# Graph layer on one core: the layers cut into five parts, merges ten chunks later, and all edge rows gathered by the POOL queue

## The chip, the core and the metric

The kernel runs on one core of a Trainium2 chip. The core has five engines with instruction queues of their own: PE (TensorE, matrix products), DVE (VectorE, elementwise work and reductions), ACT (ScalarE, activations), POOL (GpSimd, here only issuer of indirect DMAs) and SP (SyncE, here only issuer of plain DMAs). The metric is device time in microseconds, the median of the runs; lower is better. Before the change it is 1955.35 us (three runs, 1953.97 to 1955.7).

## The reference

```python
def reference(x, src, dst, Wg, Ws, bg, W1, b1, W2, b2, W3, b3):
    z = jnp.maximum(_layernorm(x, axis=-1), 0.0)        # x: 12500 x 128, fp32
    msgs = z[src]                                       # 200000 edges; src is random
    agg = segment_sum(msgs, dst, num_segments=12500)    # dst is sorted
    deg = segment_sum(ones, dst, num_segments=12500)
    agg = agg / jnp.maximum(deg, 1.0)[:, None]
    h = jax.nn.relu(agg @ Wg + z @ Ws + bg)             # 128
    h = jnp.tanh(h @ W1 + b1)                           # 512
    h = jnp.tanh(h @ W2 + b2)                           # 512
    return x + h @ W3 + b3                              # 128
```

Every edge needs one row of `z` (512 bytes), picked by `src`; the rows of edges with the same `dst` are added up.

## The kernel before

**Head (lines 120 to 274).** POOL first issues 80 indirect DMAs (line 141), each of which gathers 128 rows of the raw `x`; these 80 chunks of edges are normalised after they are gathered. Meanwhile the layer norm of all of `x` is computed and written to a table `htab` in DRAM.

**Edge loop (lines 586 to 634).** The 200000 edges are cut into 1563 chunks of 128, `c` in the loop. A chunk's rows lie in a tile of 128 x 128. `gather(c)` (line 296) is one indirect DMA on POOL that brings the 128 rows from `htab` into one of 32 tiles of the pool `rows_in` (`AHEAD = 32`), up to 32 gathered chunks ahead of the chunk in work. `onehot` builds on DVE, for eight chunks at a time, a matrix that says which of about 144 neighbouring nodes each edge belongs to. `add(c)` multiplies rows by that matrix on PE, and so sums the edges per node into PSUM. The PE queue is written out in program order (`keep_in_program_order`, line 285), and so is SP's (line 294).

**Three kinds of chunks.** 80 are the raw ones of the head. 21 are in the list `slow` (every 59th from chunk 72 on, below chunk 1376): their rows are fetched by SP, one row per DMA, 128 DMAs per chunk in batches of 16 (`row_loads`, lines 315 to 333); SP first loads the row addresses into registers, which `places` has loaded and DVE has multiplied by 512 (line 312). The other 1462 are gathered by POOL.

**Blocks.** The nodes are cut into 28 blocks: 23 of 512, then 256, 128, 128, 128 and 84. A block of 512 takes 64 chunks. Chunks whose window spans two blocks are summed into a PSUM tile `edge`, copied to SBUF by ACT (`sums`, line 427), and added to both blocks by `merge` (line 443, two matmuls with the identity). `merge(b)` stands two chunks after the block's last chunk. Then `layers(b)` (line 498) is put on the list `work`: it is a generator, and each `yield` is a step, mostly one matmul of the layers. Below chunk `QUICK = 1376` one step is taken every second chunk (line 629). From there on a small plan decides: `there` (line 612) is the time at which the plan takes the chunk's rows to be there, and layer steps that fit before it go first (lines 613 and 614). At chunk 1376 the plan's clock is far behind `there`, and so all steps left of the block in work are written out at once.

**Other inputs of the layers.** `own(s)` (line 460) loads by SP the block's rows of `x` (`xb`, three buffers) and of `htab` (`hb`, one buffer); `own_turned(s)` turns `hb` on PE. `store` issues the outputs on SP at least 12 chunks after they were computed.

Of the kernel before, what the change touches and what calls it, by code (L numbers as in the profile page):

```python
# [20 lines left out]
F32 = mybir.dt.float32  # L23
BF16 = mybir.dt.bfloat16
I32 = mybir.dt.int32
U8 = mybir.dt.uint8
AF = mybir.ActivationFunctionType
ALU = mybir.AluOpType
# [3 lines left out]
P = 128  # L32
EPS = 1e-5
CPR = 16
BLK = 512
PIECE = 14
GRP = 8
NRAW = 10
RAW0 = 256
STEP = 40  # L40
AHEAD = 32
SLOW0 = 72
EACH = 58
LOADS = 16
LATE = 12
QUICK = 1376

# [10 lines left out]
def windowed(ctx, tc, x, src, dst, Wg, Ws, bg, W1, b1, W2, b2, W3, b3, out, flag):  # L58
    nc = tc.nc
    N, D = x.shape  # L60
    (E,) = src.shape
    H = W1.shape[1]
    HM = H // P
# [6 lines left out]
    NCH = -(-E // P)  # L70
# [8 lines left out]
    def raw(c):  # L79
        return RAW0 <= c < RAW1 and (c - RAW0) % STEP < GRP  # L80


    slow, n = [], 0
    for c in range(SLOW0, QUICK):
        if not raw(c):
            if n == 0:
                slow.append(c)
                n = EACH
            else:
                n -= 1  # L90


    def first(w, span=per):
# [8 lines left out]
    blocks, n = [], 0  # L102
# [7 lines left out]
    raws = ctx.enter_context(tc.tile_pool(name="raws", bufs=1))  # L110
    rows_one = ctx.enter_context(tc.tile_pool(name="rows_one", bufs=2))
    rows_in = ctx.enter_context(tc.tile_pool(name="rows_in", bufs=AHEAD))
# [9 lines left out]
    for t, a in ((rsrc, src), (rdst, dst)):  # L122
        a = a[RAW0 * P : RAW1 * P].rearrange("(u e) -> u e", u=NRAW)[:, : GRP * P]
# [14 lines left out]
    for g in range(NRAW):  # L138
        t = raws.tile([P, GRP, D], F32, name=f"raw{g}")
# [44 lines left out]
    with tc.tile_pool(name="setup", bufs=1) as sp, tc.tile_pool(name="ln", bufs=2) as ln:  # L184
# [59 lines left out]
        for c0, w in WINDOWS[1:]:  # L244
            v = low[:, c0:]
# [47 lines left out]
    def sp_dma(*a):  # L293
        tc.keep_in_program_order(nc.sync.dma_start(*a))  # L294
# [8 lines left out]

    ROWB = 4 * D
    hbytes = htab.rearrange("n d -> (n d)").bitcast(U8)

    def places(c):

        ix = ed.tile([1, P], I32, name="ix", bufs=2)
        sp_dma(ix, src[c * P : (c + 1) * P].rearrange("(o p) -> o p", o=1))  # L310
        at = ed.tile([1, P], I32, name="at", bufs=2)
        nc.vector.tensor_scalar(at, ix, float(ROWB), None, op0=ALU.mult)
        return at

    def row_loads():
        nxt_at = places(slow[0])
        for i, c in enumerate(slow):
            at = nxt_at
            if i + 1 < len(slow):
                nxt_at = places(slow[i + 1])  # L320
            r = rows_one.tile([P, D], F32, name="srows")
            rows_t[c] = r
            rb = r.bitcast(U8)
            for p0 in range(0, P, LOADS):
                loads, vs = nc.values_load_multi_w_load_instructions(
                    at[:, p0 : p0 + LOADS], engines=[mybir.EngineType.SP], min_val=0, max_val=(N - 1) * ROWB,
                    skip_runtime_bounds_check_because="src holds rows of x, as the indirect DMAs take it to",
                )
                for ld in loads:
                    tc.keep_in_program_order(ld)  # L330
                for p, v in enumerate(vs, p0):
                    sp_dma(rb[p : p + 1, :], hbytes[bass.ds(v, ROWB)].rearrange("(o b) -> o b", o=1))
                yield

    def raw_stats(i):
# [124 lines left out]
    def own(s):  # L460

        n0 = s * BLK
        n = min(BLK, N - n0)
        k, whole = -(-n // P), n // P
        xb = ml.tile([P, BLK // P, D], F32, name="xb", bufs=3)
        if whole < k:
            nc.vector.memset(xb[:, whole, :], 0.0)
        if whole:
            sp_dma(xb[:, :whole, :], x[n0 : n0 + whole * P, :].rearrange("(t p) d -> p t d", p=P))
        if whole < k:  # L470
            sp_dma(xb[: n - whole * P, whole, :], x[n0 + whole * P : n0 + n, :])
        hb = ml.tile([P, BLK // P, D], F32, name="hb", bufs=1)
        sp_dma(hb[:, :k], htab[n0 : n0 + k * P, :].rearrange("(t p) d -> p t d", p=P))
        owns[s] = (hb, xb)

    def own_turned(s):

        k = -(-min(BLK, N - s * BLK) // P)
        hb, xb = owns.pop(s)
        pt = ps_t.tile([P, BLK // P, P], F32, name="pt")  # L480
        for t in range(k):
            pe.transpose(pt[:, t, :], hb[:, t, :], ident)
        hT = ml.tile([P, BLK], F32, name="hT")
        nc.scalar.copy(hT[:, : k * P], pt[:, :k, :].rearrange("p t n -> p (t n)"))
        hTs[s] = (hT, xb)

    def own_part(b):

        n0, n = blocks[b]
        whole = n // P  # L490
        xb = ml.tile([P, -(-n // P), D], F32, name=f"xs{b}", bufs=1)
        if whole:
            sp_dma(xb[:, :whole, :], x[n0 : n0 + whole * P, :].rearrange("(t p) d -> p t d", p=P))
        if n > whole * P:
            sp_dma(xb[: n - whole * P, whole, :], x[n0 + whole * P : n0 + n, :])
        xss[b] = xb

    def layers(b):


        n0, n = blocks[b]
        s, off = divmod(n0, BLK)
        hT, xb = hTs[s]
        k, whole = -(-n // P), n // P
        rest = n - whole * P
        if n != BLK:
            xb = xss.pop(b)
        mm, hop = 4 * (n / 2400 + 0.003), 0.5 + n / 1200

        size, bufs = (P, 2) if n <= P else (BLK, 1)  # L510
        yield 0, 0
# [3 lines left out]
        p0 = flat(ps_m.tile([P, 4, P], F32, name="pm"))  # L515
        pe.matmul(p0[:, :n], ws, hT[:, off : off + n], start=True, stop=False)
        yield mm, n / 90
        pe.matmul(p0[:, :n], wg, mT[:, :n], start=False, stop=True)
        h0 = ml.tile([P, BLK], F32, name="h0")
        nc.scalar.activation(h0[:, :n], p0[:, :n], AF.Relu, bias=bgc)  # L520
        yield 0, 0
        h1 = ml.tile([P, HM, size], F32, name=f"h1_{size}", bufs=bufs)
        for m in range(HM):
            yield mm, hop if m == 0 else 0
            p1 = flat(ps_m.tile([P, 4, P], F32, name="pm"))
            pe.matmul(p1[:, :n], w1[:, m * P : (m + 1) * P], h0[:, :n], start=True, stop=True)
            nc.scalar.activation(h1[:, m, :n], p1[:, :n], AF.Tanh, bias=b1c[:, m : m + 1])  # L527
        h2 = ml.tile([P, HM, size], F32, name=f"h2_{size}", bufs=bufs)
        for m in range(HM):
            p2 = flat(ps_m.tile([P, 4, P], F32, name="pm"))  # L530
            for kk in range(HM):
                yield mm, hop if m == 0 and kk == HM - 1 else 0
                pe.matmul(
                    p2[:, :n], w2[:, kk, m * P : (m + 1) * P], h1[:, kk, :n], start=(kk == 0), stop=(kk == HM - 1)
                )
            nc.scalar.activation(h2[:, m, :n], p2[:, :n], AF.Tanh, bias=b2c[:, m : m + 1])  # L536
        p3 = flat(ps_m.tile([P, 4, P], F32, name="pm"))
        for kk in range(HM):
            yield mm, hop if kk == HM - 1 else 0
            pe.matmul(p3[:, :n], w3[:, kk, :], h2[:, kk, :n], start=(kk == 0), stop=(kk == HM - 1))  # L540
        h3 = ml.tile([P, BLK], F32, name="h3", bufs=1)
        nc.scalar.activation(h3[:, :n], p3[:, :n], AF.Identity, bias=b3c)  # L542
        yield 0, 0
        yield k * 0.225, hop
# [11 lines left out]

    order = [c for c in range(NCH) if not raw(c) and c not in slow]
    loading = row_loads()
    work, done, nxt, behind = [], 0, 0, 0
# [8 lines left out]
    def soonest():  # L568
        two = work[: 2 if len(work) > 1 and work[1][3] < work[0][3] else 1]
        return min(two, key=lambda w: max(w[2], now), default=None)  # L570

    def go_on(w):
        nonlocal now
        if w:
            now = max(now, w[2]) + w[1]
            w[1:] = *next(w[0], (None, 0)), w[3] + 1
            w[2] += now
            if w[1] is None:
                work.remove(w)
# [6 lines left out]
    for c in range(NCH):  # L586
# [15 lines left out]
        while nxt < len(order) and nxt < behind + AHEAD:  # L602
            gather(order[nxt])
            nxt += 1
        if not raw(c) and c not in slow:
            behind += 1
            batch = behind * P // (EACH * LOADS)
            if behind > SLOW0 - 2 * EACH and batch > (behind - 1) * P // (EACH * LOADS):
                next(loading, 0)
        if c >= QUICK:  # L610

            there = 12.0 + 1.25 * (NRAW * GRP + order.index(c)) if c not in slow else 0
            while soonest() and max(now, soonest()[2]) < there:
                go_on(soonest())
            now = max(now, there) + 0.27
        add(c)

        if done < len(blocks) and (c - 2 if across[done] else c) == reach[done][-1]:
            if across[done]:
                merge(done)  # L620
            work.append([layers(done), 0, 0, 0])
            done += 1
# [391 lines left out]
```

## Time and profile before

| what | value |
|---|---|
| median of three runs | 1955.35 us |
| the profiled execution's own time | 1952.27 us |
| its span, first to last instruction | 1950.5 us (1.77 us lie around it) |
| PE busy, matmuls | 1354.8 us (69%), 5213 instructions |
| DVE busy | 1069.7 us (55%) |
| ACT busy | 231.8 us (12%) |
| POOL busy | 1458.0 us (75%), 1550 instructions |
| indirect gathers of rows, on POOL | 1462, 944 ns each |
| single-row loads, on SP | 2688, 0.5 KB each |
| mean granted PE clock | 0.916 |

A matmul in fp32 shows as two instructions in the profile. "Idle before" is the time that an engine stood still just ahead of an instruction, and the releaser is what ended it; "issue" means that nothing which the profile shows was waited for. The chain that ended last is followed back from the last instruction to whatever released each step.

### The profile page before, as it was taken

The page shows a single profiled execution, that of the slowest core. Times are in us where ns is not written, and L with a number is a line of the kernel's source. Part 1 is how long each engine was busy: PE and PEld are TensorE (multiplying, and loading weights), DVE is VectorE, ACT ScalarE, POOL GpSimd, SP SyncE. Part 2 cuts the span into 40 slices and gives each one's busy share as a digit, 9 for nine tenths or more (in the row PEclk, how much of TensorE's full clock was granted, in tenths as well). Part 3 has the DMA queues.
Part 4 walks back from the last instruction along what each step waited for, and adds up shares of the span by engine and source line. Part 5 has one row for each costly group of instructions (what it writes and reads, how often), then busy time and mean ns, then how long its engine had stood idle before and what let it go on. Part 6 is the DMA issues. An engine that isn't in the chain of part 4 may idle for free.

```text
span 1950.5 us, 20753 instructions
## 1 busy us (share of the span) xinstructions
PE 1354.8 (69%) x5213; PEld 803.5 (41%) x5213; DVE 1069.7 (55%) x671; ACT 231.8 (12%) x364; POOL 1458.0 (75%) x1550
## 2 busy tenths in 40 slices
PE   0057387778787787776676677677776676778797
PEld 0034253444454444433333334343343343454466
DVE  7874874655666566645445445455455454545430
ACT  1100211101111011101011001010110101101122
POOL 7777777777777777777777777777777777777774
PEclk9999689899899989999999998989889889868797
DMA  7822222222222222222222222222222222222221
GB/s 199 231 77 65 54 70 54 70 65 60 71 70 71 64 60 70 70 54 71 70 54 70 54 71 70 54 71 65 60 70 54 71 70 53 77 69 61 55 63 38
DMA packets 125595, 139.78 MB, mean 72 GB/s; under 512 B 33169, under 2 KB 99958, under 8 KB 125272
## 3 DMA queue, kind: packets, MB, share of 16 engines
q0 software_dynamic: 49344, 101.16, 20.5%
q1 hardware_dynamic: 72962, 33.90, 6.3%
q10 hardware_dynamic: 3160, 3.31, 0.6%
q8 instruction: 43, 0.70, 0.2%
q14 instruction: 86, 0.70, 0.1%
HBM read 125.43 MB, written 12.82 MB: 71 GB/s over the span
## 4 chain that ended last, share of the span: by engine, by line
issue 36%; DMA 26%; PE 24%; POOL 11%; DVE 1%; ACT 0%; SPq 0%; POOLq 0%; DVEq 0%; ACTq 0%
DMA rows<-htab,scol 26%; PE pm L285 12%; PE agg L285 8%; POOL rows L298 7%; POOL raw L141 4%; PE edge L285 3%; PE pt L288 1%; DVE oh L362 0%; DVE shared L171 0%; DVE raw L172 0%; DVE shared L175 0%; ACT sq L174 0%; DMA raw<-in_x_dram,rsrc 0%; SPq L294 0%; DVE rd L399 0%
## 5 line engine op out<-in xcount | busy, mean ns | idle before, releaser
L298 POOL DMA_INDIRECT rows<-htab,scol x1462 | 1379.5, 944 | 445.8 <-issue 293.4
L285 PE MATMUL agg<-oh,rows 128*128 128x144 f32 (+3 forms) x2096 | 543.9, 358 | 331.5 <-DMA rows<-htab,scol 327.7
L285 PEld LDWEIGHTS agg<-oh,rows 128*128 128x128 f32 x2096 | 369.4, 217 | 711.4 <-DMA rows<-htab,scol 595.0
L285 PE MATMUL pm<-h,w 128*128 128x512 f32 (+3 forms) x1344 | 614.1, 553 | 0.2
L362 DVE TENSOR_TENSOR oh<-shared,dloc 128x1152 f32<-128x1152 f32 (+2 forms) x186 | 245.2, 1322 | 622.5 <-PE agg L285 420.3
L372 DVE TENSOR_REDUCE cnt<-oh 128x200 bf16<-128x1600 f32 (+2 forms) x186 | 523.6, 2825 | 7.9 <-DMA htab<-h 3.6
L285 PE MATMUL edge<-oh,rows 128*128 128x144 f32 (+2 forms) x828 | 211.9, 347 | 131.3 <-DMA rows<-htab,scol 130.4
L285 PEld LDWEIGHTS edge<-oh,rows 128*128 128x128 f32 x828 | 139.8, 206 | 264.6 <-DMA rows<-htab,scol 216.9
L285 PEld LDWEIGHTS pm<-h,w 128*128 128x128 f32 x1344 | 212.7, 197 | 11.8 <-issue 9.8
L536 ACT ACTIVATE h<-pm,b2c 128x512 f32<-128x512 f32 (+3 forms) x112 | 70.8, 632 | 649.1 <-PE pm L285 649.1
L141 POOL DMA_INDIRECT raw<-in_x_dram,rsrc x80 | 77.6, 970 | 25.5 <-issue 23.8
L527 ACT ACTIVATE h<-pm,b1c 128x512 f32<-128x512 f32 (+3 forms) x112 | 70.2, 632 | 182.1 <-PE pm L285 181.5
L399 DVE RECIPROCAL rd<-rd 128x512 f32<-128x512 f32 (+3 forms) x28 | 81.8, 2920 | 0.0
L513 DVE TENSOR_TENSOR mT<-agg,rd 128x512 f32<-128x512 f32 (+3 forms) x28 | 17.3, 619 | 90.5 <-PE agg L285 90.5
L200 PE MATMUL pm<-ident,idx_f 98*128 98x98 f32 x32 | 6.2, 376 | 76.3 <-DVE agg L179 42.7
L285 PE MATMUL agg<-sums,ident 128*128 128x140 f32 (+3 forms) x108 | 28.4, 412 | 27.5 <-ACT sums L427 27.5
L397 DVE TENSOR_SCALAR rd<-pm 128x512 f32<-128x512 f32 (+3 forms) x28 | 17.4, 621 | 52.4 <-PE pm L285 52.4
L520 ACT ACTIVATE h<-pm,bgc 128x512 f32<-128x512 f32 (+3 forms) x28 | 17.7, 632 | 236.4 <-PE pm L285 236.4
L542 ACT ACTIVATE h<-pm,b3c 128x512 f32<-128x512 f32 (+3 forms) x28 | 17.7, 632 | 184.5 <-PE pm L285 184.5
L285 PE MATMUL pm<-hT,ws 128*128 128x512 f32 (+3 forms) x56 | 38.6, 784 | 0.0
L285 PEld LDWEIGHTS agg<-sums,ident 128*128 128x128 f32 x108 | 25.4, 309 | 28.3 <-ACT sums L427 28.3
L200 PEld LDWEIGHTS pm<-ident,idx_f 98*128 98x128 f32 x32 | 5.1, 223 | 77.1 <-issue 42.9
(70 smaller groups left out, 497.4 us busy)
## 6 DMA issues: line engine op xcount, KB each, us to landing
srows<-htab SPq DMA_DIRECT2D x2688, 0.5 KB
rows<-htab,scol POOLq DMA_INDIRECT x1462
xb<-in_x_dram SPq DMA_DIRECT2D x24, 256.0 KB
hb<-htab SPq DMA_DIRECT2D x24, 256.0 KB
out_dram<-o SPq DMA_DIRECT2D x23, 256.0 KB
htab<-h SPq DMA_DIRECT2D x6, 896.0 KB
xt<-in_x_dram SPq DMA_DIRECT2D x5, 896.0 KB
raw<-in_x_dram,rsrc POOLq DMA_INDIRECT x80
```

Source lines behind the costliest of these rows:

```text
L141: nc.gpsimd.indirect_dma_start(out=t[:, j, :], out_offset=None, in_=x, in_offset=bass.IndirectOffsetOnAxis(ap=rsrc[:, g, j : j + 1], axis=0),)
L285: tc.keep_in_program_order(nc.tensor.matmul(*a, **k))
L288: tc.keep_in_program_order(nc.tensor.transpose(*a, **k))
L298: nc.gpsimd.indirect_dma_start(out=r, out_offset=None, in_=htab, in_offset=bass.IndirectOffsetOnAxis(ap=scol[:, c : c + 1], axis=0),)
L362: nc.vector.tensor_tensor(oh[:, :k, :w], lane[:, None, :w].to_broadcast([P, k, w]), dloc[:, g * GRP : g * GRP + k][:, :, None].to_broadcas ...
L372: nc.vector.tensor_reduce(cnt[:, :n], shifted, AX.X, ALU.add)
L397: nc.vector.tensor_scalar(rd[:, :m], dg[:, :m], 1.0, None, op0=ALU.max)
L399: nc.vector.reciprocal(rd[:, :m], rd[:, :m])
L520: nc.scalar.activation(h0[:, :n], p0[:, :n], AF.Relu, bias=bgc)
L527: nc.scalar.activation(h1[:, m, :n], p1[:, :n], AF.Tanh, bias=b1c[:, m : m + 1])
L536: nc.scalar.activation(h2[:, m, :n], p2[:, :n], AF.Tanh, bias=b2c[:, m : m + 1])
L542: nc.scalar.activation(h3[:, :n], p3[:, :n], AF.Identity, bias=b3c)
```

## The change

- The list `slow`, `places` and `row_loads` go: SP loads no rows. All 1483 chunks that are not raw are gathered by POOL, in the same order, with the same 32 tiles.
- `layers` is cut into five parts: `part0` (the mean, `ws`, `wg`, relu), `part1` (`w1`), `part2` (`w2`), `part3` (`w3`) and `part4` (turn back, add `x`, hand the store on). For a block that is done well before chunk 1376, the order is part 0 of this block, part 3 of the block before, part 1, part 4 of the block before, part 2. Later blocks go through all five parts in a row; the first of them starts with what is left of the block before.
- `merge` and the start of the layers come ten chunks after the block's last chunk (`LEAD = 10`) rather than two; from chunk 1376 on still two.
- `xb` is loaded when `part0` starts (`own_part`) instead of with `hb`, with two buffers instead of three.
- The plan's arrival time from chunk 1376 on is 7.5 + 1.251 per gather instead of 12.0 + 1.25, and two blocks are in work side by side only where the first is a quick one of at most 128 nodes.

```diff
-SLOW0 = 72
-EACH = 58
-LOADS = 16
 LATE = 12
+LEAD = 10
...
-    rows_one = ctx.enter_context(tc.tile_pool(name="rows_one", bufs=2))
...
-    def places(c):
...
-    def row_loads():
...
-                for p, v in enumerate(vs, p0):
-                    sp_dma(rb[p : p + 1, :], hbytes[bass.ds(v, ROWB)].rearrange("(o b) -> o b", o=1))
-                yield
...
-        xb = ml.tile([P, BLK // P, D], F32, name="xb", bufs=3)
...
+        if n == BLK:
+            xb = ml.tile([P, BLK // P, D], F32, name="xb")
+        else:
+            xb = ml.tile([P, -(-n // P), D], F32, name=f"xs{b}", bufs=1)
...
+    def layers(b, before):
+        part = lambda f, *a: lambda: f(*a)
+        last = [] if before is None else [part(part3, before), part(part4, before)]
+        if reach[b][-1] + LEAD < QUICK:
+            return one_by_one(
+                part(part0, b), *last[:1], part(part1, b, True), *last[1:], part(part2, b)
+            )
+        return one_by_one(
+            *last, part(part0, b), part(part1, b, False), part(part2, b), part(part3, b), part(part4, b)
+        )
...
-    order = [c for c in range(NCH) if not raw(c) and c not in slow]
-    loading = row_loads()
+    order = [c for c in range(NCH) if not raw(c)]
...
-        two = work[: 2 if len(work) > 1 and work[1][3] < work[0][3] else 1]
+        two = work[: 2 if len(work) > 1 and work[1][3] < work[0][3] and work[0][4] else 1]
...
-            there = 12.0 + 1.25 * (NRAW * GRP + order.index(c)) if c not in slow else 0
+            there = 7.5 + 1.251 * (NRAW * GRP + order.index(c))
...
-        if done < len(blocks) and (c - 2 if across[done] else c) == reach[done][-1]:
+        lead = LEAD if c < QUICK else 2
+        if done < len(blocks) and (c - lead if across[done] else c) >= reach[done][-1]:
             if across[done]:
                 merge(done)
-            work.append([layers(done), 0, 0, 0])
+            quick = reach[done][-1] + LEAD >= QUICK
+            before = done - 1 if done and reach[done - 1][-1] + LEAD < QUICK else None
+            work.append([layers(done, before), 0, 0, 0, quick and blocks[done][1] <= P])
             done += 1
```

More of the change, by code (lines that the diff above doesn't have):

```diff
@@ L25 @@
 I32 = mybir.dt.int32
-U8 = mybir.dt.uint8
 AF = mybir.ActivationFunctionType
@@ L80, in raw @@
         return RAW0 <= c < RAW1 and (c - RAW0) % STEP < GRP
[L83 to L90, printed above, removed]
     def first(w, span=per):
@@ L302, in gather @@
         rows_t[c] = r
-    ROWB = 4 * D
-    hbytes = htab.rearrange("n d -> (n d)").bitcast(U8)
-    def places(c):
[L309 to L313, printed above, removed]
-    def row_loads():
[L316 to L330, printed above, removed]
-                for p, v in enumerate(vs, p0):
-                    sp_dma(rb[p : p + 1, :], hbytes[bass.ds(v, ROWB)].rearrange("(o b) -> o b", o=1))
-                yield
     def raw_stats(i):
@@ L463, in own @@
         n = min(BLK, N - n0)
-        k, whole = -(-n // P), n // P
-        xb = ml.tile([P, BLK // P, D], F32, name="xb", bufs=3)
[L466 to L471, printed above, removed]
+        k = -(-n // P)
         hb = ml.tile([P, BLK // P, D], F32, name="hb", bufs=1)
         sp_dma(hb[:, :k], htab[n0 : n0 + k * P, :].rearrange("(t p) d -> p t d", p=P))
-        owns[s] = (hb, xb)
+        owns[s] = hb
     def own_turned(s):
         k = -(-min(BLK, N - s * BLK) // P)
-        hb, xb = owns.pop(s)
+        hb = owns.pop(s)
         pt = ps_t.tile([P, BLK // P, P], F32, name="pt")
@@ L484, in own_turned @@
         nc.scalar.copy(hT[:, : k * P], pt[:, :k, :].rearrange("p t n -> p (t n)"))
-        hTs[s] = (hT, xb)
+        hTs[s] = hT
     def own_part(b):
@@ L490, in own_part @@
         whole = n // P
-        xb = ml.tile([P, -(-n // P), D], F32, name=f"xs{b}", bufs=1)
+        if n == BLK:
+            xb = ml.tile([P, BLK // P, D], F32, name="xb")
+        else:
+            xb = ml.tile([P, -(-n // P), D], F32, name=f"xs{b}", bufs=1)
         if whole:
@@ L496, in own_part, with costs, wide, part0 @@
         xss[b] = xb
[L498 to L510, printed above, removed]
+    h0s, h1s, h2s, h3s = {}, {}, {}, {}
+    def costs(b):
+        n = blocks[b][1]
+        return n, 4 * (n / 2400 + 0.003), 0.5 + n / 1200
+    def wide(b):
+        return (P, 2) if blocks[b][1] <= P else (BLK, 1)
+    def part0(b):
+        n, mm, hop = costs(b)
+        s, off = divmod(blocks[b][0], BLK)
+        if n == BLK:
+            own_part(b)
         yield 0, 0
@@ L515, in layers, with part1 @@
         p0 = flat(ps_m.tile([P, 4, P], F32, name="pm"))
-        pe.matmul(p0[:, :n], ws, hT[:, off : off + n], start=True, stop=False)
+        pe.matmul(p0[:, :n], ws, hTs[s][:, off : off + n], start=True, stop=False)
         yield mm, n / 90
         pe.matmul(p0[:, :n], wg, mT[:, :n], start=False, stop=True)
[L519 to L522, printed above, removed]
+        h0s[b] = ml.tile([P, BLK], F32, name="h0")
+        nc.scalar.activation(h0s[b][:, :n], p0[:, :n], AF.Relu, bias=bgc)
+    def part1(b, spread):
+        n, mm, hop = costs(b)
+        size, bufs = wide(b)
+        h0, h1s[b] = h0s.pop(b), ml.tile([P, HM, size], F32, name=f"h1_{size}", bufs=bufs)
         for m in range(HM):
+            if spread and m > 1:
+                yield 0, 0
             yield mm, hop if m == 0 else 0
@@ L526, in layers, with part2 @@
             pe.matmul(p1[:, :n], w1[:, m * P : (m + 1) * P], h0[:, :n], start=True, stop=True)
-            nc.scalar.activation(h1[:, m, :n], p1[:, :n], AF.Tanh, bias=b1c[:, m : m + 1])
-        h2 = ml.tile([P, HM, size], F32, name=f"h2_{size}", bufs=bufs)
+            nc.scalar.activation(h1s[b][:, m, :n], p1[:, :n], AF.Tanh, bias=b1c[:, m : m + 1])
+    def part2(b):
+        n, mm, hop = costs(b)
+        size, bufs = wide(b)
+        h1, h2s[b] = h1s.pop(b), ml.tile([P, HM, size], F32, name=f"h2_{size}", bufs=bufs)
         for m in range(HM):
@@ L535, in layers, with part3 @@
                 )
-            nc.scalar.activation(h2[:, m, :n], p2[:, :n], AF.Tanh, bias=b2c[:, m : m + 1])
+            nc.scalar.activation(h2s[b][:, m, :n], p2[:, :n], AF.Tanh, bias=b2c[:, m : m + 1])
+    def part3(b):
+        n, mm, hop = costs(b)
+        h2 = h2s.pop(b)
         p3 = flat(ps_m.tile([P, 4, P], F32, name="pm"))
@@ L540, in layers, with part4 @@
             pe.matmul(p3[:, :n], w3[:, kk, :], h2[:, kk, :n], start=(kk == 0), stop=(kk == HM - 1))
-        h3 = ml.tile([P, BLK], F32, name="h3", bufs=1)
-        nc.scalar.activation(h3[:, :n], p3[:, :n], AF.Identity, bias=b3c)
-        yield 0, 0
+        h3s[b] = ml.tile([P, BLK], F32, name="h3", bufs=1)
+        nc.scalar.activation(h3s[b][:, :n], p3[:, :n], AF.Identity, bias=b3c)
+    def part4(b):
+        n0, (n, mm, hop) = blocks[b][0], costs(b)
+        k, whole = -(-n // P), n // P
+        rest = n - whole * P
+        xb, h3 = xss.pop(b), h3s.pop(b)
         yield k * 0.225, hop
@@ L555, in layers, with one_by_one @@
             stores.append((at, out[n0 + whole * P : n0 + n, :], o[:rest, whole, :]))
-    order = [c for c in range(NCH) if not raw(c) and c not in slow]
-    loading = row_loads()
+    def one_by_one(*parts):
+        for part in parts:
+            yield from part()
+    def layers(b, before):
[9 more added lines that the diff above has]
+    order = [c for c in range(NCH) if not raw(c)]
     work, done, nxt, behind = [], 0, 0, 0
@@ L575, in go_on @@
             now = max(now, w[2]) + w[1]
-            w[1:] = *next(w[0], (None, 0)), w[3] + 1
+            w[1:4] = *next(w[0], (None, 0)), w[3] + 1
             w[2] += now
@@ L604, in windowed @@
             nxt += 1
[L605 to L609, printed above, removed]
+        behind += not raw(c)
         if c >= QUICK:
-            there = 12.0 + 1.25 * (NRAW * GRP + order.index(c)) if c not in slow else 0
+            there = 7.5 + 1.251 * (NRAW * GRP + order.index(c))
             while soonest() and max(now, soonest()[2]) < there:
```

## The prediction

> **What bounds the kernel now.** I read the page first, then POOL's waits, then the gathers alone, then the last microseconds in order of time. The page, with the busy tenths of POOL in 40 slices, the gathers' row (busy and mean ns, then idle before them) and SP's row loads:
>
> ```profile
> span 1950.5 us, 20753 instructions
> ...
> POOL 7777777777777777777777777777777777777774
> ...
> L298 POOL DMA_INDIRECT rows<-htab,scol x1462 | 1379.5, 944 | 445.8 <-issue 293.4
> ...
> srows<-htab SPq DMA_DIRECT2D x2688, 0.5 KB
> ```
>
> POOL is at the same seven tenths from the first slice to the last but one. An engine that waits for others now and then does not look like that. POOL's waits (total, times, longest) say what its idle time is:
>
> ```profile
> POOL rows L298 <- issue: 293.4, 962, 0.3
> POOL rows L298 <- PE agg L285: 61.0, 200, 0.3
> POOL rows L298 <- DMA rows<-htab,scol: 35.4, 116, 0.3
> ```
>
> The longest is 0.3 us whatever the name beside it: this is the gap that stands ahead of every gather, not a wait. So gathers leave at a fixed pace, and PE waits for them (327.7 + 130.4 us for rows, in PE's waits). The pace, from the first and the last gather in order of time:
>
> ```profile
> 104.94 0.95 POOL L298 DMA_INDIRECT rows<-htab,scol  x1 [0.30 <-issue]
> 1928.98 0.94 POOL L298 DMA_INDIRECT rows<-htab,scol  x1 [0.31 <-POOLq L980]
> ```
>
> (1928.98 - 104.94) / 1461 = 1.2485 us. POOL's chain of 80 raw and 1462 row gathers sets when the last rows come; 1950.5 - 1928.98 = 21.52 us of tail follow.
>
> **Part 1: SP's row loads go.** SP is freed of 2688 issues of 227 ns, 610 us, and DVE of 21 products of 217 ns, 4.5 us. Neither is on the path: PE waited for such rows 0.8 us in all. Gain 0. Could their going make POOL's gathers cheaper? The trace of before has both conditions, since SP's loads run from 107.7 to 1619.2:
>
> ```profile
> L294 SPq DMA_DIRECT2D srows<-htab x2688: 227/228/314, 107.7 to 1619.2; - x192
> ```
>
> ```profile
> core 0: us, POOL busy (x), PEclk, DMA share, GB/s
> 107.40:1699.20 1591.80, 1202.97 (x1275) 0.93 0.25 65
> 1699.20:1929.93 230.73, 174.55 (x185) 0.80 0.24 61
> ```
>
> With them 1202.97 / 1275 = 943.5 ns per gather and 1591.80 / 1275 = 1.2485 us of pace; without them 174.55 / 185 = 943.5 ns, and 184 starts from 1699.29 to 1928.98 give 1.2483 us. The bound on a gain is the difference, 0.2 ns x 1482 = 0.3 us. I take 0.
>
> **Part 2: 21 more gathers.** Nothing is taken from POOL, and in the built order of instructions its queue holds 80 and then 1483 gathers. The first row gather stays at 104.94, since the raw ones stand ahead of it. The last starts at 104.94 + 1482 x 1.2485 = 1955.2: **26.2 us later**, all on the path.
>
> A rule speaks against this price. The Trainium skill, DMA: Bandwidth & Descriptors, section "Issuing engines are not separate DMA queues", says that starting DMAs from several engines saves only the time to initiate them, usually small beside the transfer; by it the return of 21 chunks to POOL would cost close to nothing and the profiled time stay near 1952. The rows above decide against "small": initiating is the pace of this kernel.
>
> **Part 3: merges ten chunks later.** Once, the merge stalled PE:
>
> ```profile
> PE agg L285 <- ACT sums L427: 27.5, 1, 27.5
> ```
>
> This is block 0's merge, 199.7 to 227.2: the copy to `sums` stood in ACT's queue behind squares of raw chunks, the last at 225.78. In the built order after, that copy stands behind five of those squares instead of nine, and its merge eight chunks (10 us) later, so most of the 27.5 us go. They are worth nothing to the end, since POOL's gathers kept their 0.3 us gaps through the stall: the 32 tiles cover 32 x 1.2485 = 40 us from a gather to the reuse of its tile, less 2.5 us for landing (the DMA pieces of the chain), 37.5 us. Afterwards PE did four chunks in 2.13 us. Bounds: 27.5 gained if PE set the end, 0 by POOL's gaps; I take 0.
>
> **Part 4: the layers in parts.** Counts and widths of the matmuls stay (28 with `ws`, 28 with `wg`, 672 with the other weights, 54 merges), and a block still takes 30 steps of the 32 that its 64 chunks offer. The new waits: `part1` is now behind `part3` of the block before, so the relu has four more matmuls to finish in; `part4` has half of `part1` ahead of it, so h3 is there. The one large lump is at chunk 1376, where all steps left are written out: 18 matmuls of 512 and four turns before, 1698.48 to 1715.53, 17.0 us. After it is 21, because the block starts eight chunks later: 3 x 0.87 = 2.6 us more (15.61 us / 18 = 0.87 each), 19.6 us, inside 37.5. Cost 0; if the cover were gone, what exceeds 37.5 us.
>
> **Part 5: SP's queue.** The 23 loads of `xb` for full blocks move from ahead of `hb` to the start of `part0`, and can wait there for `part4` of two blocks before (two buffers). That stands in the layers of the block before and is done by then. Queued behind are a store, which nobody waits for, and the next `hb`, needed for the turn 42 chunks (52 us) after its place. A DMA row of SP costs 0.4 to 0.5 us to issue. Cost 0, covered by those 52 us and then by POOL's 37.5.
>
> **Part 6: the tail.** The plan's arrival of the last rows was 12.0 + 1.25 x 1541 = 1938.3 against about 1928.98 + 2.5 = 1931.4 true, 6.8 late; it is 7.5 + 1.251 x 1562 = 1961.6 against 1957.7, 3.9 late. In the built orders PE has 2560 columns more layer work left after the lump than before (five matmuls of 512, 4.3 us), but 100 chunks from the end the two are equal, and over the last 25 chunks they agree step by step. So the tail stays:
>
> ```profile
> 1934.17 0.30 PEld L285 LDWEIGHTS agg<-oh,rows 128*128 128x128 f32 x2
> ...
> 1937.36 5.79 PE L285 MATMUL pm<-h,w 128*128 128x84 f32 x48
> ...
> 1943.91 0.29 DVE L554 TENSOR_TENSOR o<-pt,xs 84x128 f32<-84x128 f32 x1 [6.12 <-PE pt L288]
> ```
>
> The last rows land at 1931.4 and are used at 1934.2, so at most 2.7 us can be gained. At worst the clock is low in the last layers: ten 128-wide layer instructions took 2.50 us at 1907.53 and 1.52 at 1911.33; 5.79 x (2.50 / 1.52 - 1) = 3.7 us lost. I take 0, as the order of instructions is the same. The granted clock, by windows, is 0.50 from 1725 to 1750 and 1.00 from 1850 to 1900, so both rates do occur. The Trainium skill, TensorE: Matmul & The Clock Gate, Part 1 ("The HAM clock gate"), lets PE run at full or at half rate by how busy it was; by half rate those 5.79 us would cost 5.8 more.
>
> **Sum.** 1952.27 + 26.2 = 1978.5 for an execution like the profiled one. That one lies 3.1 us under the median of the runs; against the median it is 1955.35 + 26.2 = 1981.6. I give 1981.
>
> **Rivals.**
> - *PE's stalls did set the end, not slower.* The one place is block 0's merge. If POOL had been held through it, the 27.5 us would come back and the time be 1981.6 - 27.5 = 1954.1, no change. It decides from 22.3 us of POOL held there (26.2 less 3.9). For it: PE is the busiest but one and waits 27.5 us at once. Against: no gap of POOL over 0.31 us among 1462.
> - *Gathers get cheaper without SP's queue.* Break-even at 26.2 / 1562 = 17 ns per gather, time 1955. Against: 943.5 ns in both windows above.
> - *PE falls behind by more than the cover.* If a stall of 27.5 and a lump of 19.6 us met, 47.1 - 37.5 = 9.6 us of POOL wait, 1991. For it: the order of ACT and DVE around the raw chunks is new. Against: they lie 1400 us apart.
> - *The change does not do it.* Excluded: the built queues hold 1483 row gathers and no row loads.
>
> **How the numbers follow.** My case 0.92, PE behind 0.04, PE's stall 0.02, cheaper gathers 0.02. The range is my own case's, from 1978.5 - 2.7 = 1975.8 (fast execution, short tail) to 1981.6 + 3.7 = 1985.3 (median, slow tail); it leaves out the rivals and little of my case. About 0.2% (3.9 us) is what a measurement of this kernel can tell from no change. Slower: 0.96, my case and PE behind; same 0.02; faster 0.02, cheaper gathers past break-even.
>
> **What would show it.** Right: 1483 gathers of 944 ns, no gap over 0.4 us, the first at 104.9, the last near 1955.2, a tail of 19 to 25 us, the 27.5 us wait for `sums` shorter and the time not better for it. Wrong: a pace under 1.24 us, a POOL wait of microseconds by PE, or a last gather off 1955 by more than 2.

## The result and the profile after

The changed kernel takes 1980.51 us (median of four runs, 1977.2 to 1980.86) against 1955.22 us before (four runs, 1953.97 to 1955.7): 1.0125 times as long, 95% interval 1.0111 to 1.0139, 25.3 us slower. The profiled execution took 1977.2 us, its span is 1975.4.

The page of the changed kernel, with the busy tenths of POOL in 40 slices and the gathers' row (busy and mean ns, then idle before them):

```profile
span 1975.4 us, 15009 instructions
...
POOL 7777777777777777777777777777777777777774
...
L283 POOL DMA_INDIRECT rows<-htab,scol x1483 | 1399.2, 944 | 452.0 <-issue 283.1
```

POOL's waits (total, times, longest) still know nothing but the gap ahead of each gather:

```profile
POOL rows L283 <- issue: 283.1, 929, 0.3
POOL rows L283 <- PE agg L270: 70.1, 230, 0.3
POOL rows L283 <- DMA rows<-htab,scol: 48.5, 159, 0.3
```

The first and the last row gather of the changed kernel, in order of time:

```profile
104.63 0.94 POOL L283 DMA_INDIRECT rows<-htab,scol  x1 [0.31 <-issue]
...
1954.57 0.94 POOL L283 DMA_INDIRECT rows<-htab,scol  x1 [0.30 <-PE pm L270]
```

(1954.57 - 104.63) / 1482 = 1.2483 us per gather. The last one starts 25.59 us later than before (1928.98): 21 gathers make 26.22, the first came 0.31 earlier, and 1482 paces of 0.2 ns less give some 0.32 back. Behind it lie 1975.4 - 1954.57 = 20.83 us, 0.69 less than before. 25.59 - 0.69 = 24.9 us, the difference of the spans.

PE's longest waits after are these (total, times, longest); the 27.5 us for `sums` of before are gone, and the time is not better for it:

```profile
PE agg L270 <- DMA rows<-htab,scol: 331.8, 509, 5.2
PE edge L270 <- DMA rows<-htab,scol: 126.7, 179, 1.8
PE pm L185 <- DVE agg L164: 42.3, 1, 42.3
```

### The profile page after: what moved, and what is told of

Read it like the earlier page. It is cut to its first block, busy times and chain, and to the rows that moved or that the text cites. A ratio compares the mean times of both kernels' runs of the same rounds, so it can differ in the third digit from the quotient of the medians.

```text
span 1975.4 us, 15009 instructions
## 1 busy us (share of the span) xinstructions
PE 1404.7 (71%) x5213; PEld 823.1 (42%) x5213; DVE 1067.8 (54%) x649; ACT 231.4 (12%) x364; POOL 1477.4 (75%) x1571
## 4 chain that ended last, share of the span: by engine, by line
DMA 33%; issue 32%; PE 24%; POOL 10%; ACT 0%; DVE 0%; POOLq 0%; ACTq 0%; DVEq 0%
DMA rows<-htab,scol 33%; PE pm L270 12%; PE agg L270 8%; POOL rows L283 7%; POOL raw L126 4%; PE edge L270 2%; PE pt L273 1%; DMA raw<-in_x_dram,rsrc 0%; DVE oh L316 0%; ACT h L474 0%; DVE shared L160 0%; ACT sq L159 0%; DMA rsrc<-in_src_dram 0%; POOLq L283 0%; ACT h L509 0%
## 5 line engine op out<-in xcount | busy, mean ns | idle before, releaser
L283 POOL DMA_INDIRECT rows<-htab,scol x1483 | 1399.2, 944 | 452.0 <-issue 283.1
L270 PE MATMUL agg<-oh,rows 128*128 128x144 f32 (+3 forms) x2120 | 574.1, 368 | 337.3 <-DMA rows<-htab,scol 331.8
L270 PEld LDWEIGHTS agg<-oh,rows 128*128 128x128 f32 x2120 | 387.9, 224 | 727.2 <-DMA rows<-htab,scol 624.5
L270 PE MATMUL pm<-h,w 128*128 128x512 f32 (+3 forms) x1344 | 630.3, 565 | 1.4 <-ACT h L474 1.2
L523 DVE TENSOR_TENSOR o<-pt,xb 128x512 f32<-128x512 f32 x23 | 15.9, 690 | 99.2 <-PE pt L273 99.2
L431 ACT COPY hT<-pt 128x512 f32<-128x512 f32 (+1 forms) x25 | 14.4, 577 | 260.6 <-PE pt L273 260.6
```

What stands on the lines that cost most here:

```text
L270: tc.keep_in_program_order(nc.tensor.matmul(*a, **k))
L283: nc.gpsimd.indirect_dma_start(out=r, out_offset=None, in_=htab, in_offset=bass.IndirectOffsetOnAxis(ap=scol[:, c : c + 1], axis=0),)
```

## The experiments

Theory: POOL's fixed pace times the number of its gathers sets the end, and the order of layers and merges moves nothing as long as PE stays within the 32 tiles. Rivals: the new order gives something back, or costs something; or PE's stalls set the end.

One thing must be known first. The experiments fell on four chips; on which one the change itself was measured is not on record. Beside the change and on the chip of the second pair of runs (`e5` and `e6`), the kernel before took 1955.2 and 1951.5 us. On the other three chips it took 2465.3, 2467.9 and 2503.6, with the same program. There engines stand still, again and again, for something that the profile books as "remote" (an unknown queue) or as "issue". This is ACT and PE of the first run below, in order of time; ACT could have gone on when the matmul before it was done, at 359.2, and starts 12.9 us later:

```profile
372.13 0.69 ACT L520 ACTIVATE h<-pm,bgc 128x512 f32<-128x512 f32 x1 [20.12 <-remote]
372.87 0.50 PEld L285 LDWEIGHTS pm<-h,w 128*128 128x128 f32 x2 [12.92 <-issue]
372.87 2.08 PE L285 MATMUL pm<-h,w 128*128 128x512 f32 x2 [12.71 <-issue]
```

PE's 12.7 us are not a stop of its own: it needs the `h` that ACT writes until 372.82, and the profile's "issue" hides that. What keeps ACT there was not found. I call these the halting chips, and compare within a chip only. Each of them was seen at one time only, so whether the chip itself or something that ran beside it makes the difference is not shown.

**Each half of the change, first on a halting chip.** `e1_gathers_alone` is the kernel before without SP's row loads:

```diff
-    for c in range(SLOW0, QUICK):
+    for c in ():
...
-    loading = row_loads()
+    loading = iter(())
```

> The kernel before, with the list of SP's chunks empty and nothing else changed: layers, merges and plan as before, 1483 gathers on POOL. POOL's pace sets the end (my theory): the last gather starts at 104.8 + 1482 x 1.2483 = 1954.8, the 27.5 us stall of block 0's merge is still there and costs nothing, and the time is that of the changed kernel, 1980.5 (1979 to 1983). If the new order of layers and merges had given something back that the 21 gathers took, this kernel is slower than the changed one by that much: up to 27.5 us, 2008. If it had cost something, this kernel is faster than the changed one.

`e2_parts_alone` is the changed kernel with the code of `slow`, `places` and `row_loads` put back:

```diff
-    order = [c for c in range(NCH) if not raw(c)]
+    order = [c for c in range(NCH) if not raw(c) and c not in slow]
+    loading = row_loads()
...
-            there = 7.5 + 1.251 * (NRAW * GRP + order.index(c))
+            there = 7.5 + 1.251 * (NRAW * GRP + order.index(c)) if c not in slow else 0
```

> The changed kernel with SP's row loads put back: five parts, merges ten chunks later and the new plan, but 1462 gathers on POOL and 21 chunks loaded by SP. My theory: last gather at 1928.7, no gap of POOL over 0.4 us, the merge stall gone and the time that of the kernel before, 1955 (1953 to 1957). If PE's stalls set the end, it is faster, down to 1955 - 27.5 = 1928. If the new order costs, it is slower than 1957.

Two more let SP load more chunks, on the kernel before (`EACH = 46` instead of 58; in the second also `range(SLOW0, 1520)` instead of `range(SLOW0, QUICK)`):

> The kernel before with every 47th chunk instead of every 59th loaded by SP: 27 chunks, so 1456 gathers, six fewer. SP issues 64 such loads in 25.08 us, a chunk in 50.2, and 47 gathers last 58.7, so it keeps up. My theory: 6 x 1.2483 = 7.5 us faster than before, 1947.7 (1946 to 1950). If something else than the number of gathers sets the end, no change, 1955. If SP falls behind by more than the 37.5 us that the 32 tiles cover, POOL waits and it is slower than 1950.

> As the run before, but SP's chunks go on beyond chunk 1376 to chunk 1515: 30 chunks, 1453 gathers, nine fewer than before. My theory: 9 x 1.2483 = 11.2 us faster than before, 1944 (1942 to 1947). Rival: behind chunk 1376 SP's queue holds output stores that wait for the layers, row loads stand behind them, PE gets its rows late and the tail grows: then no faster than the run before, 1947.7, or slower.

Measured, against 2465.32 before on this chip (medians; the ratios, here and below, are taken over the runs and differ from the quotient of the medians by up to 0.3%): gathers alone 2293.14, ratio 0.9295 (0.925 to 0.934); parts alone 2481.03, 1.0051 (1.0022 to 1.0081); 27 chunks by SP 2742.61, 1.1119 (1.1058 to 1.1179); 30 chunks 2785.2, 1.1298 (1.124 to 1.1357). All four expectations of time missed, and the sign is turned round: here SP's row loads cost time. SP's issues say why. The first line is of the kernel before on its own chip, the second of the parts alone on the halting one, 64 row loads each (the parts alone on the chip of `e6` show 25.18 us in such a line):

```profile
442.97 25.08 SPq L294 DMA_DIRECT2D srows<-htab  x64
```

```profile
427.44 42.64 SPq L294 DMA_DIRECT2D srows<-htab  x64
```

0.39 us per row load became 0.67, so a chunk of 128 takes SP 85 us instead of 50. One such load still lasts 228 ns in the median on both chips; its longest went from 314 to 1397 ns, so some are held up, and most are not. POOL is slower there as well: in the gathers alone its row gathers start from 122.65 to 2251.23, 1.4363 us each, so 58 of them last 83.3 us (72.4 on the chip of the change) and 46 last 66. SP's loads ran from 131.8 to 2130.2 for 21 chunks (95 us each, waits included), from 131.3 to 2457.1 for 27 (86 each) and from 132.5 to 2706.9 for 30 (86 each). With a chunk for every 46 gathers SP is clearly the bound, and more chunks for it made it worse; with one for every 58 it falls behind by little, and POOL's pace in the parts alone is 1.5794 us, from 122.60 to 2430.05. How SP holds POOL is seen in the parts alone:

```profile
456.93 0.94 POOL L298 DMA_INDIRECT rows<-htab,scol  x1 [0.30 <-issue]
...
471.54 0.82 PE L285 MATMUL edge<-oh,srows 128*128 128x144 f32 x2 [26.59 <-DMA ix<-in_src_dram]
...
474.82 0.94 POOL L298 DMA_INDIRECT rows<-htab,scol  x1 [16.94 <-PE edge L285]
```

PE waits 26.6 us for the rows of chunk 190, which SP loads (the product reads `srows`; the `ix` that the profile names is another load of SP's); POOL goes on until its tiles are full and then stands 16.9 us. The gather that is held is the 221st of rows; 188 chunks with gathered rows stand ahead of chunk 190, and 188 + 32 = 220 are out. Most of the other long gaps of POOL lie a multiple of 58 gathers behind this one, as SP's chunks do. This is the rival "PE falls behind by more than the cover", in a form that the prediction had not thought of.

Where waits just before it, for SP's rows among them, have used the cover up, block 0's merge does reach POOL. In the run with 27 chunks by SP, which has 32 tiles and the merges of before, PE waits for `sums`, and POOL's 107th row gather waits for PE:

```profile
296.12 1.30 PE L285 MATMUL agg<-sums,ident 128*128 128x140 f32 x4 [19.57 <-ACT sums L427]
```

```profile
298.17 0.94 POOL L298 DMA_INDIRECT rows<-htab,scol  x1 [19.63 <-PE agg L285]
```

So the theory's condition, "as long as PE stays within the 32 tiles", is a real one: here PE was past them, and the stall cost POOL its full length.

**Each half again, on a chip that does not halt.** The same two kernels.

> Again the kernel before with the list of SP's chunks empty and nothing else changed, on another chip: on the first one every engine, the kernel before too, stood still for up to 18 us at a time without a cause in the kernel. My theory as before: the last gather starts at 1954.8, the stall of block 0's merge is still there, and the time is 25.3 us over that of the kernel before, as the changed kernel's (1979 to 1983). If the order of layers and merges gave something back, this is slower than the changed kernel by that, up to 2008.

> Again the changed kernel with SP's row loads put back (1462 gathers on POOL, 21 chunks by SP, five parts, merges ten chunks later, new plan). My theory: last gather at 1928.7, the merge stall gone, and the time that of the kernel before within 2 us, 1955. If PE's stalls set the end it is faster, down to 1928; if the new order costs, slower than 1957.

Measured, against 1951.46 before on this chip: gathers alone 1978.26, ratio 1.0135 (1.0118 to 1.0152), 26.8 us slower; parts alone 1949.84, 0.9991 (0.9982 to 1.0001), 1.6 us less and not clear of nothing. Both lie within 2 us of what was expected, counted from the kernel before on this chip. The two add up to 25.2, and the change cost 25.3 where it was measured. POOL's last gather of the gathers alone, then of the parts alone:

```profile
1954.45 0.94 POOL L298 DMA_INDIRECT rows<-htab,scol  x1 [0.30 <-PE pm L285]
```

```profile
1928.63 0.94 POOL L298 DMA_INDIRECT rows<-htab,scol  x1 [0.30 <-POOLq L1019]
```

They stand where the number of gathers puts them, 1483 and 1462, whatever the order of layers. In both, no gap ahead of a row gather is over 0.32 us. And the stall at block 0's merge did not follow the merges, which both expectations had wrong. Among PE's waits of the parts alone, with merges ten chunks later, it is there; in the gathers alone, with merges as before, it is not:

```profile
PE agg L285 <- ACT sums L427: 16.9, 1, 16.9
```

The copy to `sums` runs behind nine squares of raw chunks on ACT in both kernels with SP's row loads and behind five in both without. These are the copies of the parts alone and of the gathers alone:

```profile
226.43 0.37 ACT L427 COPY sums<-edge 128x280 f32<-128x280 f32 x1
```

```profile
197.89 0.39 ACT L427 COPY sums<-edge 128x280 f32<-128x280 f32 x1 [10.93 <-PE edge L285]
```

So it was the row loads in the program that put the copy late in ACT's queue; the later merge took 10.6 of the 27.5 us off, no more. Stalls of 27.5, 16.9 and none leave the longest gap ahead of a row gather at 0.3 us in all four kernels that were traced where nothing halts.

**How far the tiles carry.** Both kernels with `AHEAD = 16` instead of 32, the one before twice; all three fell on halting chips.

> The kernel before with 16 tiles for gathered rows instead of 32. The cover is then 16 x 1.2483 - 2.5 = 17.5 us instead of 37.5. ACT's order is as before, so block 0's merge still stalls PE 27.5 us; that is 10 us over the cover. My theory: POOL waits some 10 us for PE once, near 215 to 227, and the time is 10 us over that of the kernel before (8 to 12). If POOL is not held by full tiles, or catches up, no change. If PE falls behind in many places, the time grows by tens of us.

> The changed kernel with 16 tiles instead of 32. It has no stall at block 0's merge; its largest lump, at chunk 1376, was estimated at 19.6 us, 2 over the cover of 17.5. My theory: 25.3 + 2 = 27 us over the kernel before with 32 tiles (25 to 29); so with 16 tiles the change costs some 17 us instead of 25, and the order of ACT is worth 8 to 10 us there. If PE's order never matters, the two kernels stay 25 apart.

> Again the kernel before with 16 tiles for gathered rows instead of 32, hoped on a chip whose engines do not stand still. Cover 16 x 1.2483 - 2.5 = 17.5 us, block 0's merge stalls PE 27.5 us. My theory: POOL waits some 10 us for PE once, near 215 to 227, and the time is 10 us (8 to 12) over that of the kernel before. If full tiles do not hold POOL, no change; if PE falls behind in many places, tens of us.

Measured: before with 16 tiles 2485.25 against 2467.87, ratio 1.0058 (1.0028 to 1.0088), and on another chip 2514.41 against 2503.55, 1.0042 (1.0013 to 1.007); after with 16 tiles 2282.71 against 2467.87, 0.925 (0.9202 to 0.9297). None of the three expected times came out. The 10 us that I expected at one stall can't be told from the times, since SP held PE at every chunk of its own. The traces show the stall: in the second run (`e12`) PE waits 14.57 us for `sums`, and POOL's 91st row gather waits 14.64 us for PE:

```profile
277.69 0.94 POOL L298 DMA_INDIRECT rows<-htab,scol  x1 [14.64 <-PE agg L285]
```

Here, too, PE had waited for a chunk of SP's just before, 17.02 us. The traces also settle the number of tiles. In the same run POOL stood here, at the 205th row gather, the first beyond 188 + 16, for the same chunk 190:

```profile
441.51 0.94 POOL L298 DMA_INDIRECT rows<-htab,scol  x1 [0.30 <-issue]
454.48 0.94 POOL L298 DMA_INDIRECT rows<-htab,scol  x1 [12.03 <-PE edge L285]
```

Most of the other long gaps lie 16 gathers earlier than in the parts alone with 32 tiles, too. What a stall of 27.5 us costs with 16 tiles on a chip that does not halt stays open, as does the exact length of the cover in us.

**Does PE's work set anything?** Three of four matmuls of the `w2` layer are left out of the changed kernel:

```diff
-                pe.matmul(
-                    p2[:, :n], w2[:, kk, m * P : (m + 1) * P], h1[:, kk, :n], start=(kk == 0), stop=(kk == HM - 1)
-                )
+                if kk == HM - 1:
+                    pe.matmul(
+                        p2[:, :n], w2[:, kk, m * P : (m + 1) * P], h1[:, kk, :n], start=True, stop=True
+                    )
```

> The changed kernel with three of four matmuls of the w2 layer left out (h1 of the last quarter alone goes into p2), so its output is not the reference's; PE has 336 matmuls less, by 0.87 us for the 512-wide ones some 280 us. My theory: the last gather starts at 1954.6 as before and only the tail shrinks, by up to 3 us, since 12 of the last block's 24 matmuls (5.79 us) go: 1974 to 1979. If PE's work set the pace of the kernel, the time falls by tens of us.

Measured on a halting chip, one run: 2279.32 us. The nearest thing on the same chip is the changed kernel with 16 tiles, 2282.71. PE was busy 282 us less (the page's first lines; 1405.2 in the other), and the time is 3.4 us apart, less than the four runs of the other differ among themselves (2269.54 to 2288.39):

```profile
PE 1122.8 (49%) x4541; PEld 789.8 (35%) x4541; DVE 1057.4 (46%) x649; ACT 228.6 (10%) x364; POOL 1479.5 (65%) x1571
```

The expected 1974 to 1979 could not come out on that chip. That 282 us of PE's work change the time by so little speaks against PE's amount of work as the pace even there; it is one run, and the two kernels differ in tiles as well, so this is support and no proof.

**What a gather costs.** The changed kernel with 21 more gathers, of half the rows:

```diff
+        if c in again:
+            half = spare.tile([P // 2, D], F32, name="half")
+            nc.gpsimd.indirect_dma_start(
+                out=half, out_offset=None, in_=htab,
+                in_offset=bass.IndirectOffsetOnAxis(ap=scol[: P // 2, c : c + 1], axis=0),
+            )
```

> The changed kernel with 21 more gathers, of 64 rows each, into tiles that nobody reads, one behind each of the 21 chunks that SP had loaded. If a gather costs by the instruction, each adds 1.248 us and the time grows by 26.2 us; if it costs by the row, each adds half of 0.944 and the gap of 0.30, 0.77 us, and the time grows by 16.2 us. In both theories POOL sets the end; if it does not, the time stays.

The half gathers did not run where the expectation puts them: POOL did all 21 between 216.6 and 313.5 us, several in a row. Measured: 2326.6 us, one run on a halting chip, which says nothing about the price. The durations do, since a full gather lasts 943 to 945 ns in the mean in every run. The half ones (minimum, median, maximum in ns), and two that follow each other:

```profile
L303 POOL DMA_INDIRECT half<-htab,scol x21: 893/903/907, 216.6 to 313.5; - x21
...
275.01 0.90 POOL L303 DMA_INDIRECT half<-htab,scol  x1 [0.30 <-issue]
276.22 0.90 POOL L303 DMA_INDIRECT half<-htab,scol  x1 [0.30 <-issue]
```

64 rows cost 903 ns, 128 rows 944, and from start to start 1.21 us against 1.248. If the cost is a straight line through these two, an estimate, 862 ns belong to the instruction and 0.64 ns to a row. So of the two theories it is cost by the instruction: half the rows make a gather only 41 ns shorter.

**More chunks by SP on the new order.** `e2_parts_alone` with `EACH = 46` and chunks up to 1515, meant as a kernel that beats both:

> The changed kernel with SP's row loads put back and more of them: every 47th chunk up to chunk 1515, 30 chunks by SP, 1453 gathers. My theory, on a chip whose engines do not stand still without a cause: 9 gathers less than the kernel before, 9 x 1.2483 = 11.2 us, and up to 1.6 us of the shorter tail seen with the parts alone: 11 to 13 us faster than before. Rival: SP, at 50.2 of every 58.7 us with rows, falls behind at its stores behind chunk 1376 and the tail grows: less than 8 us faster. On a chip whose engines stand still, SP's loads set the end and it is some 10% slower, as with the runs of that kind on the first chip.

Measured on a halting chip: 2822.55 against 2503.55, ratio 1.1248 (1.1183 to 1.1312). The part of the expectation for such a chip (some 10% slower) came true. Whether it gains 11 us elsewhere stays open.

## Why the prediction was right, point by point

- **The bound and part 2.** 26.2 us were forecast for 21 gathers, all on the path. The last gather came 25.59 us later, and the gathers alone cost 26.8 us in the medians. The forecast rests on this one term. That 1981 lies within half a microsecond of 1980.51 is partly luck. For the profiled execution the sum gave 1978.5, and it took 1977.2: the first gather came 0.31 us earlier, the pace gave 0.32 us and the tail 0.69, all three taken as 0.
- **The rule weighed.** The Trainium skill (DMA: Bandwidth & Descriptors, "Issuing engines are not separate DMA queues") calls the time to initiate a DMA usually small beside the transfer; by that the return to POOL would have been nearly free. The measurement decides: where starting the DMAs is itself the pace, giving up the second issuer cost 26.8 us of 1951.46. On a halting chip the same step gained 172 us, since there POOL stood at SP's chunks.
- **Part 1, cheaper gathers.** That 943.5 ns stay the same without SP's loads held: the changed kernel's gathers last 944 ns in the mean, and its pace is 1.2483 us against 1.2485.
- **Part 3, the merges.** The price, 0, was right, and so was that the stall goes. Its cause was wrong: the stall's going was counted under the later merges. The parts alone show that the place came with the removal of the row loads, and that the later merge alone leaves 16.9 us.
- **Part 4, the lump at chunk 1376.** Estimated 19.6 us. In order of time after:

```profile
1724.07 4.46 PE L270 MATMUL pm<-h,w 128*128 128x512 f32 x10
...
1742.53 5.33 PE L270 MATMUL agg<-oh,rows 128*128 128x144 f32 x38
```

It lasted 1742.53 - 1724.07 = 18.5 us: the 17.0 us taken from before hold a wait of 0.78 us of PE for h3, and in the profile after there is none ahead of the turn, which has four `w1` matmuls before it. That is most of the difference. Nothing came of it, as POOL shows.
- **Part 6, the tail.** Order the same, length 20.83 instead of 21.52, inside the bounds of 2.7 less and 3.7 more. (The 1.52 us in the second bound start at 1911.41 on PE; 1911.33 is their weight load.) The clock is a part of what moves it. In all four traces the granted clock goes from 0.50 to 1.00 inside the tail. In the last but one block, the second group of ten layer instructions took 1.62 us before, 1.56 after, 2.07 in the gathers alone and 1.36 in the parts alone; the tails are 21.52, 20.83, 21.85 and 19.87, in the same order. It is not all: of the 1.65 us between before and the parts alone, 0.91 lie ahead of the last turn (14.59 and 13.68 us behind the last gather) and 0.74 behind it (6.93 and 6.19 us, in which the output is stored). These are single executions from two sets of runs, and where the 1.6 us of the parts alone come from is not shown.
- **The profiled execution against the median** was 3.1 us low before and 3.3 us low after, so to work from the median was right.
- **The rival of PE behind the tiles** was given 0.04 and 1991 us. On the chip of the forecast it had no part. On the halting chips it had: POOL stood for PE, which stood for SP's rows, in every trace there of a kernel with SP's loads. On two of them the sign was turned: 0.9295 for the gathers alone, and 0.925 for the changed kernel with 16 tiles. The changed kernel itself was not measured there. The forecast had no term for the chip.

## What to carry to other kernels

Where one engine issues without a real wait from start to end, count its instructions: work moved to or from it costs its pace times the count, and reorderings elsewhere are worth nothing while the buffers between cover them. A second issuer that is near its own limit is a gain only as long as it keeps up: at 50 us per chunk it bought 26 us, at 85 us, on a halting chip, it cost 172. If a reordering seems to remove a stall, test it alone: the built order can move for another reason in the same change.

## What the runs showed of the hardware that was not expected

- An indirect gather of 64 rows lasts 903 ns, one of 128 rows 944; with the gap of 0.30 us that makes a pace of 1.248 us for the full one. The mean duration of a full one is 943 to 945 ns in every run, whatever the chip.
- The same program took 1951 to 1955 us in two sets of runs and 2465 to 2504 us in three, on three other chips. On those, engines stand still, 12.9 us in the line shown, with a releaser that the profile does not know, and a row load of SP in a run of 64 takes 0.67 us instead of 0.39. The gathers alone, without the 2688 row loads, lost 16% there (1978 to 2293), the kernel before 26%. Why is open.
